# Regrouping the blocks of a feed-forward layer that is woven into a gather loop

## The chip, the cores and the metric

The kernel runs on one core of one Trainium2 chip. The metric is device time in microseconds (us) of one execution, compared as the median of several runs; less is better. TensorE (PE in the profile) multiplies matrices, with its weight loads shown apart (PEld); VectorE is DVE, ScalarE is ACT, GpSimd is POOL, and SyncE is SP. Each engine works through its own queue in order, and semaphores tie the queues together.

## The reference, cut to what matters

Two layers, each a graph convolution and a mixture of experts with residuals, run over 6,250 nodes of 256 features and 100,000 edges. Only the second layer ("layer 1") is touched:

```python
x = x + _L1_gnn_ref(edge_index, _layernorm(x), edge_type_8, L1_gnn_weight, ...)   # sum over the edges
# of a node: hx[edge_type, src], plus a loop term
x = x + _L1_ffn_ref(_layernorm(x)[None], ...)
# _L1_ffn_ref, per node: rh = relu(f @ router_w1 + b); p = softmax(rh @ router_w2 + b)
#   top 2 of 6 experts, their p put through a second softmax
#   expert e: relu(relu(f @ w1[e] + b1) @ w2[e] + b2) @ w3[e] + b3, all matrices 256 x 256
#   output: the two chosen experts, weighted
```

The kernel computes all six experts for every node, and weights those not chosen with zero.

## The kernel before, in words

The 6,250 nodes lie in 49 blocks of 128. X (the features) and acc (the sums of the graph convolution) stay in the on-chip memory for all 49 blocks. The stages follow one another: the edges are sorted into tiles, layer 0's convolution and experts run, the table hx of layer 1 (each node times eight relation matrices, as three bf16 parts) is written to HBM, and then layer 1's last stage runs, which is the one that the change touches.

**The gather loop.** `aggregate` (L801) takes T = 830 turns. In each, POOL issues one indirect DMA (L815) that fetches 128 rows of hx into one of ten buffers g; PE multiplies them, in three matmuls (L823), with a 0/1 matrix m that DVE builds once for eight turns (L807); DVE adds the product to the block of acc (L827). Edges are ordered by their target, so blocks become complete one after another: by the bound that the program uses, block b is complete at turn 17 x (b+1) + 8 (TURNS = 17, SLACK = 8).

**The feed-forward, woven in.** `aggregate` is a generator that yields once per turn, and `layer1` (L1395) uses each yield to put other work in the queues. The 49 blocks are split into groups by SIZES (L48); before the change these are a group of 2, eleven groups of 4, a group of 2 and a group of 1. A group passes through two generators:

- `prepare` (L1306), about one step per yield: residual and statistics of a block (L1313, L1317, one block per step), the inverse root (L385 to L392), normalising and transposing (L1329, L416, L418), the router's first product pq (L1339, with ACT's relu into q, L1341), the router's second product pl (L1346), softmax, the choice of two and the second softmax, a chain of some 25 small DVE rows with two exponentials on ACT (L1351, L865 to L897) that ends in the weights C, the transposes pc of C (L1360) with ACT's copy cT (L1362), and one product pcb per block that adds the weighted last bias (L1367, L1368). For four blocks this is 24 steps, for two 19, for one 15 or so.
- `experts1` (L1373): for each of six experts, two hidden products of two halves (L428, tiles ph_e1 and ph_e2, each half a piece, followed by ACT's relu, L435), and then `mix` (L904, L905), a product py for each block with the weighted add to X, two blocks to a piece. So an expert has 4 pieces plus one per two blocks: 36 pieces in a group of four, 30 in a group of two and also in a group of one.

A group's preparation may begin when its last block is complete and fewer than two groups wait in `queue`. Pieces of the experts are dealt out by a running account: each turn adds left / (T - turn + 40) to `due`, capped at 1.5, and a piece is issued for each whole unit; `left` begins as the pieces of all groups but the last two. When `queue` is empty no piece can be issued. After turn 830 what is left is issued at full rate, one step and one piece at a time.

**Order.** Every engine's queue is fixed when the program is built. A transpose, pq, pl or pc stands in PE's one queue among the gather's matmuls and the pieces, and if its input is late, everything behind it waits.

The same loop is built twice: the branch with names ending in b is for inputs with uneven blocks, the branch with names ending in a is the one that this input takes (all tiles of the trace end in a).

Of the kernel before, what the change touches and what calls it, by code (L numbers as in the profile page):

```python
# [44 lines left out]
TABLE_GROUPS = [(0, 1)] + [(g, 4) for g in range(1, NT, 4)]  # L45

LIVE = 3
SIZES = [2] + [4] * 11 + [2, 1]  # L48
FFN_GROUPS = [(sum(SIZES[:i]), n) for i, n in enumerate(SIZES)]


@with_exitstack
def gnn_ffn_kernel(ctx: ExitStack, tc: tile.TileContext, a, out):
# [747 lines left out]
    def aggregate(pool, acc, table, tag):  # L801

        for t0 in range(0, TL, 8):
            n = min(8, T - t0)
            blocks = blocks_of(blkd, t0, [ENG.DVE], NT)
            m = pool.tile([128, 8, 128], BF16, name=f"m1{tag}_{t0}", tag="m", bufs=2)
            nc.vector.tensor_tensor(  # L807
                m[:, :n],
                lanes_h[:, None, :].to_broadcast([128, n, 128]),
                dlocT[:, t0 : t0 + n, None].to_broadcast([128, n, 128]),  # L810
                OP.is_equal,
            )
            for j in range(n):
                g = pool.tile([128, 3 * D], BF16, name=f"g1{tag}_{t0 + j}", tag="g", bufs=10)
                nc.gpsimd.indirect_dma_start(  # L815
                    out=g,
                    out_offset=None,
                    in_=table,
                    in_offset=bass.IndirectOffsetOnAxis(ap=idxT[:, t0 + j : t0 + j + 1], axis=0),
                )  # L820
                ps = psum_mm(f"pa1{tag}_{t0 + j}")
                for k in range(3):
                    nc.tensor.matmul(  # L823
                        ps[:, :D], m[:, j, :], g[:, k * D : (k + 1) * D], start=(k == 0), stop=(k == 2)
                    )
                here = acc[:, bass.ds(blocks[j] * D, D)]
                nc.vector.tensor_add(here, here, ps[:, :D])  # L827
                yield t0 + j + 1
# [544 lines left out]
    def experts1(g, n, va, tag, xT, C):  # L1373

        tiles = range(g, g + n)
        m = n * 128
        for e in range(6):
            h1 = va.tile([128, 2, 512], F32, name=f"v1{tag}_{g}_{e}", tag="actT", bufs=1)
            h2 = va.tile([128, 2, 512], F32, name=f"v2{tag}_{g}_{e}", tag="hid", bufs=1)
            b1 = [col("L1_ffn_expert_b1", 2 * e + f) for f in range(2)]  # L1380
            b2 = [col("L1_ffn_expert_b2", 2 * e + f) for f in range(2)]
            yield from dense_steps(f"e1{tag}_{g}_{e}", vw1[:, e], xT, m, AF.Relu, b1, h1)
            yield from dense_steps(f"e2{tag}_{g}_{e}", vw2[:, e], h1, m, AF.Relu, b2, h2)
            for i, t in enumerate(tiles):
                mix(f"1{tag}", t, i, e, C, h2, i * 128, vw3[:, e])
                if e == 5:
                    r = last if t == NT - 1 else 128
                    nc.sync.dma_start(out[t * 128 : t * 128 + r, :], X[:r, t, :])
                if i % 2 or i == n - 1:
                    yield  # L1390

    def pieces(n):
        return 6 * (4 + (n + 1) // 2)

    def layer1(tag, early):  # L1395


        with tc.tile_pool(name=f"gather{tag}", bufs=1) as gp, tc.tile_pool(name=f"act{tag}", bufs=1) as va:
            waiting = list(FFN_GROUPS)
            prep, queue = None, []  # L1400
            left = sum(pieces(n) for _, n in waiting[:-2])

            def prepare_some():

                nonlocal prep
                if prep is None:
                    return False
                g, n, steps = prep
                try:
                    next(steps)  # L1410
                except StopIteration as end:
                    queue.append(experts1(g, n, va, tag, *end.value))
                    prep = None
                return True

            def experts_some():
                while queue:
                    if next(queue[0], queue) is not queue:
                        return True
                    queue.pop(0)  # L1420
                return False

            due = 0.0
            for turn in aggregate(gp, acc, hx, tag):
                if not early:
                    continue
                if prep is None and waiting and len(queue) < LIVE - 1 and TURNS * sum(waiting[0]) + SLACK <= turn:
                    g, n = waiting.pop(0)
                    prep = (g, n, prepare(g, n, va, tag))
                prepare_some()  # L1430
                due = min(due + left / (T - turn + 40), 1.5)
                while due >= 1 and experts_some():
                    due, left = due - 1, left - 1
            while prep or waiting or queue:
                if prep is None and waiting and len(queue) < LIVE:
                    g, n = waiting.pop(0)
                    prep = (g, n, prepare(g, n, va, tag))
                prepare_some()
                experts_some()

    nlate_v = nc.values_load(nlate[0:1, 0:1], min_val=0, max_val=NT, skip_runtime_bounds_check_because="it is a count")
    with tc.If(nlate_v > 0) as late_cmp:
        layer1("b", False)
    with late_cmp.Else():
        layer1("a", True)
# [56 lines left out]
```

## Time and profile before

| what | value |
|---|---|
| median of 3 runs | 4212.74 us (4209.37 to 4214.22) |
| the profiled execution, its own time | 4220.04 us |
| its span, first to last instruction | 4218.3 us |
| busy, PE / PEld / DVE / ACT / POOL | 3288.1 / 2125.4 / 2072.4 / 1168.6 / 2307.8 us |
| mean granted TensorE clock | 0.883 |
| first and last gather of layer 1 issued (L815) | 2955.8 and 4095.2 us |
| last add of the gather loop (L827) begins | 4110.1 us |
| last product of the experts (L904) begins | 4212.3 us |
| PE busy, DMA share, stretch 3300 to 3400 us | 99.76 of 100 us, 0.55 |

Busy times are of one profiled execution, which was 7.3 us above the median. A row of a list of instructions gives its start and its duration; xN means N records merged in the row. A float32 product leaves two records, so a 128x512 half of a hidden layer (two products) is x4. In brackets stand the idle time of the engine before the row and what ended it.

### The profile page before, as it was taken

The numbers are of one execution on the slowest core, as the hardware profiler recorded it, in microseconds if no ns is written. First come the engines' busy times: TensorE is split into PE (matmuls) and PEld (weight loads), VectorE is DVE, ScalarE is ACT, GpSimd is POOL, SyncE is SP. The second block draws the span as 40 slices with busy tenths as digits, with TensorE's granted clock in tenths as the row PEclk, the third lists the DMA queues.
The fourth block names the chain that finished last, engine by engine and source line by source line (L and its number), as shares of the span: only waits on it lengthen the run. The fifth ranks groups of instructions, "written<-read, shape, count | busy, mean of one in ns | idle before, by whom it ended". The sixth has DMA issues, their size and how long they took to land.

```text
span 4218.3 us, 49934 instructions
## 1 busy us (share of the span) xinstructions
PE 3288.1 (78%) x13207; PEld 2125.4 (50%) x13207; DVE 2072.4 (49%) x5527; ACT 1168.6 (28%) x2569; POOL 2307.8 (55%) x2488
## 2 busy tenths in 40 slices
PE   2886555565555559999749977999679999999999
PEld 1565444444444335554537743444256666666656
DVE  5676200000000058888563357665456666666652
ACT  3312433333333300000434433665012222222213
POOL 1000777777777755555470048333767777777750
PEclk9998877767777779999769988999589999999999
DMA  4413433333333356666333335444655555555540
GB/s 169 155 43 110 153 124 121 123 123 120 121 122 122 108 190 230 225 227 209 106 115 107 109 105 201 194 194 205 190 142 151 152 151 153 150 155 150 146 117 9
DMA packets 235392, 611.60 MB, mean 145 GB/s; under 512 B 44269, under 2 KB 128482, under 8 KB 215139
## 3 DMA queue, kind: packets, MB, share of 16 engines
q0 software_dynamic: 102928, 294.81, 22.5%
q1 hardware_dynamic: 105200, 234.80, 16.6%
q10 hardware_dynamic: 26976, 78.69, 5.4%
q8 instruction: 115, 1.88, 0.2%
q14 instruction: 173, 1.42, 0.1%
HBM read 371.46 MB, written 243.18 MB: 146 GB/s over the span
## 4 chain that ended last, share of the span: by engine, by line
PE 42%; DVE 10%; POOL 4%; issue 3%; DMA 3%; ACT 2%; DVEq 1%; SPq 0%; POOLq 0%; ACTq 0%
PE ph_e1a L428 6%; PE py1a L904 6%; PE pa1a L823 5%; PE pa L797 5%; PE ph_e2a L428 5%; PE phx L1265 4%; DVE acc L799 3%; PE pf L1184 2%; PE pf L1200 2%; POOL m L795 2%; DVE rest L1275 1%; PE pg L989 1%; DVE acc L827 1%; PE pt_fh L416 1%; DVE hx L1259 1%
## 5 line engine op out<-in xcount | busy, mean ns | idle before, releaser
L764 POOL DMA_INDIRECT msgs<-msg,at x830 | 833.1, 1004 | 599.2 <-ACT msg L761 388.6
L815 POOL DMA_INDIRECT g1a<-hx,idxT x830 | 826.6, 996 | 321.1 <-PE pa1a L823 148.0
L758 PE MATMUL px<-acc,sT 128*128 x1660 | 601.4, 541 | 481.7 <-ACT msg L761 447.6
L758 PEld LDWEIGHTS px<-acc,sT 128*128 128x128 f32 x1660 | 459.3, 284 | 623.1 <-ACT msg L761 487.6
L761 ACT ACTIVATE msg<-px,ewT 128x256 f32<-128x256 f32 x830 | 356.7, 474 | 697.1 <-DMA msgs<-msg,at 568.6
L827 DVE TENSOR_TENSOR acc<-acc,pa1a 128x256 f32 x830 | 346.6, 418 | 341.7 <-PE pa1a L823 311.1
L797 PE MATMUL pa<-g,m 128*128 128x256 f32 x1660 | 448.2, 419 | 84.5 <-DVE m L787 44.7
L823 PE MATMUL pa1a<-g1a,m1a 128*128 128x256 bf16 x2490 | 376.4, 283 | 51.9 <-DMA g1a<-hx,idxT 37.2
L1265 PE MATMUL phx<-wr,xT 128*128 128x512 f32 x784 | 371.7, 618 | 29.2 <-DVE rest L1275 22.8
L797 PEld LDWEIGHTS pa<-g,m 128*128 128x128 f32 x1660 | 249.5, 189 | 283.5 <-issue 114.8
L795 POOL TENSOR_SCALAR m<-lanes,key 128x128 f32<-128x128 f32 x414 | 263.2, 651 | 229.0 <-PE pa L797 206.4
L799 DVE TENSOR_TENSOR acc<-acc,pa 128x256 f32 x830 | 348.2, 419 | 73.6 <-PE pa L797 6.0
L823 PEld LDWEIGHTS <-m1a 128*128 128x128 bf16 x2490 | 243.2, 100 | 277.3 <-issue 191.7
L755 DVE COPY msg<-srcT 128x32 f32<-128x32 f32 x104 | 18.8, 182 | 700.2 <-DMA msgs<-msg,at 700.0
L904 PE MATMUL py1a<-w_L_ffn_expert_w,v2a 128*128 128x256 f32 x1176 | 286.6, 384 | 6.0 <-DVE acc L827 3.0
L428 PE MATMUL ph_e1a<-xT3a,w_L_ffn_expert_w 128*128 128x512 f32 (+2 forms) x672 | 288.0, 555 | 0.0
L428 PE MATMUL ph_e2a<-v1a,w_L_ffn_expert_w 128*128 128x512 f32 (+2 forms) x672 | 280.1, 542 | 2.1 <-DVE acc L827 1.3
L1225 POOL DMA_INDIRECT y<-ys,ats x98 | 98.0, 1000 | 298.3 <-DMA ys<-fy 272.5
L435 ACT ACTIVATE v1a<-ph_e1a,cols 128x512 f32<-128x512 f32 (+2 forms) x168 | 106.5, 634 | 538.7 <-PE ph_e1a L428 538.6
L1265 PEld LDWEIGHTS phx<-wr,xT 128*128 128x128 f32 x784 | 149.1, 198 | 189.6 <-issue 163.4
L904 PEld LDWEIGHTS py1a<-w_L_ffn_expert_w,v2a 128*128 128x128 f32 x1176 | 208.8, 190 | 44.2 <-ACT v2a L435 10.1
L753 DVE TENSOR_SCALAR sT<-rows,part 128x1024 f32<-128x1024 bf16 x104 | 83.8, 808 | 236.0 <-PE px L758 233.5
(610 smaller groups left out, 4285.6 us busy)
## 6 DMA issues: line engine op xcount, KB each, us to landing
hx<-hx SPq DMA_DIRECT2D x49, 1536.0 KB, 5.0
g<-msgs SPq DMA_DIRECT2D x52, 1040.0 KB
g<-msgs ACTq DMA_DIRECT2D x52, 1040.0 KB, 4.9
rows<-lane_rows SPq DMA_DIRECT2D x104, 256.0 KB, 3.6
fx<-xs SPq DMA_DIRECT2D x105, 128.0 KB, 2.0
ys<-fy ACTq DMA_DIRECT2D x105, 128.0 KB
msgs<-msg,at POOLq DMA_INDIRECT x830
g1a<-hx,idxT POOLq DMA_INDIRECT x830
```

The lines of the kernel that those rows point to most:

```text
L428: nc.tensor.matmul(ps[:, :ncols], w[:, k, f * 128 : (f + 1) * 128], xT[:, k, :ncols], start=(k == 0), stop=(k == 1),)
L758: nc.tensor.matmul(ps[:, :D], sT[:, j, :], acc[:, bass.ds(blocks[j] * D, D)], start=True, stop=True)
L761: nc.scalar.activation(msg[:, j, :D], ps[:, :D], AF.Copy, scale=ewT[:, t0 + j : t0 + j + 1])
L764: ins = nc.gpsimd.indirect_dma_start(out=msgs, out_offset=bass.IndirectOffsetOnAxis(ap=at[:, t0 + j : t0 + j + 1], axis=0), in_=msg[:, j, ...
L795: nc.gpsimd.tensor_scalar(m[:, j], lanes, key[:, j : j + 1], None, op0=OP.is_equal)
L797: nc.tensor.matmul(ps[:, :D], m[:, j, :], g[:, j, :D], start=True, stop=True)
L799: nc.vector.tensor_add(here, here, ps[:, :D])
L815: nc.gpsimd.indirect_dma_start(out=g, out_offset=None, in_=table, in_offset=bass.IndirectOffsetOnAxis(ap=idxT[:, t0 + j : t0 + j + 1], axi ...
L823: nc.tensor.matmul(ps[:, :D], m[:, j, :], g[:, k * D : (k + 1) * D], start=(k == 0), stop=(k == 2))
L827: nc.vector.tensor_add(here, here, ps[:, :D])
L904: nc.tensor.matmul(ps[:, :D], hT[:, k, j : j + 128], w[:, k, :], start=(k == 0), stop=(k == 1))
L1265: nc.tensor.matmul(ps, xT[:, k, :], wr[:, k, r : r + 2, :].rearrange("p r o -> p (r o)"), start=(k == 0), stop=(k == 1),)
```

## The change

The groups become 1, 2, 2, 3, then nine of 4, then 2, 2 and 1: sixteen groups where there were fourteen. And in a turn in which a step of a preparation was taken while `queue` holds no group, a second step is taken.

```diff
-SIZES = [2] + [4] * 11 + [2, 1]
+SIZES = [1, 2, 2, 3] + [4] * 9 + [2, 2, 1]
...
                 if prep is None and waiting and len(queue) < LIVE - 1 and TURNS * sum(waiting[0]) + SLACK <= turn:
                     g, n = waiting.pop(0)
                     prep = (g, n, prepare(g, n, va, tag))
-                prepare_some()
+
+                if prepare_some() and not queue:
+                    prepare_some()
                 due = min(due + left / (T - turn + 40), 1.5)
                 while due >= 1 and experts_some():
                     due, left = due - 1, left - 1
```

`left` begins at 480 where it was 426, since small groups have more pieces for the same blocks.

## Prediction

> **What bounds the kernel now.** I read the page's slices first, for where PE is full:
>
> ```profile
> PE   2886555565555559999749977999679999999999
> ...
> POOL 1000777777777755555470048333767777777750
> ...
> PEclk9998877767777779999769988999589999999999
> ```
>
> Each digit is a tenth of a 105 us slice. The last 12 slices are layer 1's gather loop. In its first two slices PE is at 6 and 7 and the granted clock at 5 and 8; in the other ten both are at 9. POOL is at 6 or 7 and ends one slice before PE. So PE bounds the stage except at its head. The stretches (busy us of PE, PEld, DVE, ACT, POOL, then PE's clock, DMA share, GB/s) say by how much:
>
> ```profile
> core 0: us, PE busy (x) PEld busy (x) DVE busy (x) ACT busy (x) POOL busy (x), PEclk, DMA share, GB/s
> ...
> 2950.00:3000.00 50.00, 24.70 (x93) 9.44 (x93) 17.97 (x34) 0.00 (x0) 34.16 (x34) 0.50 0.78 248
> 3000.00:3050.00 50.00, 31.77 (x126) 16.37 (x127) 25.68 (x84) 4.15 (x9) 36.65 (x39) 0.59 0.56 154
> ...
> 3200.00:3300.00 100.00, 99.53 (x472) 62.99 (x471) 63.41 (x169) 20.83 (x34) 73.49 (x74) 1.00 0.54 151
> ...
> 4050.00:4100.00 50.00, 44.87 (x193) 26.86 (x192) 26.43 (x90) 9.05 (x17) 25.48 (x26) 0.90 0.41 118
> ...
> 4150.00:4219.00 69.00, 60.15 (x292) 46.91 (x290) 13.14 (x41) 21.71 (x53) 0.00 (x0) 0.98 0.04 14
> ```
>
> From 2955.8 us (first gather) to about 3150, PE is half idle and much of it at half clock; from 3200 on it is full; near 4075 it loses 5 us, and 9 in the last 69. What sets the pace at the head is POOL:
>
> ```profile
> 3019.78 0.95 POOL L815 DMA_INDIRECT g1a<-hx,idxT  x1 [0.30 <-issue]
> 3021.03 0.94 POOL L815 DMA_INDIRECT g1a<-hx,idxT  x1 [0.30 <-issue]
> ```
>
> The start-to-start of the gathers is 1.25 us (0.95 busy, 0.30 issue), whatever PE does. At turn 251 the 250 turns before have taken 350 us: gather 251 is issued at 3296.4, its add begins at 3306.2.
>
> **A price list for PE.** At full clock, from rows of full stretches: the three gather matmuls 0.35 us per turn; a float32 record of 128x512 0.4325, of 128x256 0.216 (128x384 by proportion, 0.324). Per block and expert that is 2.59 us, and 15.6 for six; preparation adds 1.6 per block. Laying out PE's queue by turns and pricing each row gives 817 us for turns 151 to 750 of before, which took 818.5. I count in this list and in time lost against it. Before: 1134.1 of work in the stage, and from 2955.8 to the last product's start near 4212.5 some 123 lost, nearly all of it (107) before turn 251.
>
> **Work added.** Two more groups. Their extra DVE rows (about 30 of 0.17 us each, 5 us per group), ACT relus and weight loads (0.19 us each) lie beside PE, which is the full one (DVE 63%, ACT 21%). Uncovered, DVE's would cost 10. On PE only the second group of one costs more per block:
>
> ```profile
> 4185.96 1.89 PE L428 MATMUL ph_e1a<-xT3a,w_L_ffn_expert_w 128*128 128x256 f32 x8
> 4187.68 1.92 PE L428 MATMUL ph_e2a<-v1a,w_L_ffn_expert_w 128*128 128x256 f32 x8
> 4189.74 1.99 PE L904 MATMUL py1a<-w_L_ffn_expert_w,v2a 128*128 128x256 f32 x8
> 4191.57 1.05 PE L428 MATMUL ph_e1a<-xT3a,w_L_ffn_expert_w 128*128 128x128 f32 x8
> 4192.69 1.16 PE L428 MATMUL ph_e2a<-v1a,w_L_ffn_expert_w 128*128 128x128 f32 x8
> ```
>
> In the first three rows a group of two takes 5.61 us per expert (three phases, 4185.96 to 4191.57), of which the list has 5.19; in the last two a group of one, with 128 columns, starts its next phase after 1.12 us for 8 records, 0.14 each and not 0.108. So a group of one costs 6 x (16 x 0.14 + 0.87) = 18.7 against 15.6: **+3.2**. The Trainium skill ("TensorE: Matmul & The Clock Gate", section "Wait — 56ns, not 53.3ns?") has warm matmuls start N / 2.4 GHz plus 2.5 ns apart, which would make the short records nearly proportional and this term about 0.3; the measured row decides. Gathers, SP's stores and POOL's queue keep their number and order.
>
> **The head, turns 1 to 250.** The experts now begin at turn 32 instead of 60, and the 17 turns without a piece (116 to 132), where before waited 29 us, go. But the account deals out pieces, not work. It gives 0.57 pieces per turn (480/838), and a piece is worth 18.7/30 = 0.62 us in a group of one, 1.04 in a group of two, 46.7/36 = 1.30 in the group of three, 1.73 in a group of four. So PE's load per turn is 0.35 + 0.57 x 0.62 = 0.70, then 0.94, then 1.09, each plus about 0.1 of preparation: under POOL's 1.25 until the group of three ends, at turn 250. PE cannot be filled there, POOL paces it. Gather 251 then comes at 2955.8 + 250 x 1.25 = 3268, plus delays of the gathers that no buffer explains (5.6 us in the first 125 turns of before, so 11) = 3279, and its add 10 later (3306.2 - 3296.4 in before) = 3289 to 3290. **-16.** Bounds: -23 if add follows gather by 4 us, as it does where PE waits for data, and 0 if short pieces hold PE back (a rival below). In these turns the list has 234.3 us of work after and 243.5 before, as a piece is smaller; so 9.2 is put off, and with the 3.2: **+12.4** behind turn 250.
>
> **The double step** acts only with the queue empty: in the first group (8 turns instead of 15, where POOL paces anyway) and in the gaps below. There the same DVE chain must finish with fewer gather turns standing between pl and pc; PE waits for the chain either way. I take 0, between -2 and +2 for each gap.
>
> **The gaps.** After turn 250 the account is faster than the blocks: a group of four is dealt out in 36/0.573 = 63 turns, but four blocks take 4 x 17 = 68 turns to become complete. The queue runs dry, with turns without a piece: 3 before turn 506, 4 before 572, 6 before 639, 6 before 705, 8 before 772. Before has 2 or 3 up to turn 609, then 4 (677), 4 (745), 6 (813). What such a gap costs is in the trace; the one of 6:
>
> ```profile
> 4053.58 1.88 PE L428 MATMUL ph_e1a<-xT3a,w_L_ffn_expert_w 128*128 128x512 f32 x4
> ...
> 4063.59 0.95 PE L1346 MATMUL pl3a<-qw,qa 128*128 128x6 f32 x8
> ...
> 4074.44 0.18 DVE L897 TENSOR_TENSOR C1a<-oh_1a,oh_1a 128x24 f32<-128x24 f32 x1
> 4074.68 0.60 PE L1360 MATMUL pc1a<-ident,C1a 128*6 128x128 f32 x4 [4.04 <-DVE C1a L897]
> ...
> 4075.94 1.35 PEld L1367 LDWEIGHTS pcb1a<-vb,cT1a 6*128 6x128 f32 x4 [0.96 <-ACT cT1a L1362]
> ...
> 4081.31 3.62 PE L428 MATMUL ph_e1a<-xT3a,w_L_ffn_expert_w 128*128 128x512 f32 x4
> ```
>
> pl ends at 4064.4, its chain on DVE gives C only 10 us later, and pc stands in PE's queue in front of the gathers and experts that wait: 4.04 us idle, 0.67 for cT (in its row), and then half clock: pcb 2.07 for 1.13, e1 3.62 for the 1.88 of the first row. Together with the second pcb and two gather turns at half clock: 9. The gap of 4 at 745:
>
> ```profile
> 3976.16 0.31 PEld L1360 LDWEIGHTS pc1a<-ident,C1a 128*6 128x6 f32 x4 [1.90 <-DVE C1a L897]
> ...
> 3980.49 3.40 PE L428 MATMUL ph_e1a<-xT3a,w_L_ffn_expert_w 128*128 128x512 f32 x4
> ```
>
> 1.62 and 0.66 idle, and e1 at 3.40: 4. The gap of 4 at 677 cost nothing, as two ph_e2 and two py pieces stood between pl and pc (9 us of cover).
>
> The cover decides, and PE's new order shows it. Before turn 506: two ph_e2 and four py halves between pl and pc, covered, 0. Before 572: the same queue as before 813, 8. Before 639: pl after the last py, only five gather turns between (1.75) against a chain of 6.3 (5.8 at 3873 with few adds between its rows, 10 above): 4.5 + 0.7 + 3.5 of clock = 9. Before 705: two turns, 5.6 + 0.7 + 3.5 = 9.5. Before 772: the transposes too are late, for the normalised blocks: about 2 more idle and pq at half clock, 13. Sum 39.5, against 13 before: **+26** (from +8, if half of each is hidden, to +40 if all chains take 10). In the row at 3980 the clock is halved after 2.3 us of idle. The skill (same page, "HAM oscillation — how this bites in real kernels") has it fall only for idle gaps over about 3.4 us; by the page the gap before 572 might keep its clock and the sum be 3 lower.
>
> **The tail.** The loop ends with 26 of 30 pieces of a group of two, and a two and a one, instead of 24 of 36 of a four, a two and a one. The work is in the list; the waits for ACT between phases, 0.42 per expert of a two, now come 11 times, not 6: **+2**.
>
> Sum: -16 + 12.4 + 26 + 2 = +24. The profiled execution's 4220.04 becomes 4244; it lay 7.3 above the median, so on the median of 4212.74 I forecast 4237.
>
> **Rivals.** *Faster:* the head keeps POOL's bare pace (-22) and the double step lets the chains end under the gather turns, so that the gaps cost 10 in all, 3 less than before: -22 + 12.4 - 3 + 2 = -11, 4202. It decides for faster once the gaps cost under 12 with the head at -22. For it: 116 to 132, the worst stall of before, is certainly removed. Against: 6 us of chain against 0.7 to 2 of cover.
>
> *No change:* gaps as at 745, 4 each, one covered: 16, so +3, and the head at -16: +1, 4214.
>
> *Slower still:* short pieces at half clock hold PE behind POOL. A piece of a group of one, four records at twice 0.14, is then 1.1 us; the 1.7 gather turns to a piece, at twice 0.35, are 1.2; and where before ran a group of two (3055 to 3110) PE waited some 0.56 for ACT after many a piece. That is 2.9 us against 2.1 of POOL, and over the group's 30 pieces 23 late, of which the ten buffers take up 7 (add 11 behind gather instead of 4). The head then gains nothing, 4253, or 6 if the clock rises half way, 4247.
>
> That the other branch runs is excluded by the names of the trace.
>
> **How the numbers follow.** Forecast 0.58 (its own range 4222 to 4247), slower still 0.12, no change 0.17, faster 0.13. 0.2% is 8.4 us, about what a measurement of this kernel can tell from no change. Faster by more than that: 0.13; within it: 0.17 and the low edge of the forecast, 0.19; slower: 0.68. The range that leaves out a tenth at each end goes from the faster rival, 4202, to 4257, where the head gains nothing and the gaps cost 4 more.
>
> **What would show it.** Right: add 251 near 3290; PE under 90% busy up to about turn 250; pc rows with 4 to 6 us idle before C, followed by e1 rows near 3.4, four of them between turns 565 and 775; the last gather later than 4095, near 4130, and a tail after it shorter by about 15. Wrong: PE full between turns 560 and 775, or no half-clock rows there; or a gather pace above 1.3 us before turn 250.

## The result, and the profile after

The changed kernel takes 4258.32 us (median of 5 runs, 4254.02 to 4259.44), the kernel before 4212.74 on the same chip: a ratio of 1.0105 (95% interval 1.0093 to 1.0117), 45.6 us slower. The forecast was 4237, slower, in a range from 4202 to 4257; the median lies 1.3 us above that range's upper end. The sign held, but the loss forecast, 24 us, was about half of the one that came. All experiments below ran on three other chips, where the kernel before takes 4528.58 us (e1 to e4), 4499.84 (e5 to e8) and 4532.24 (e9 to e12), so they are read as ratios to the kernel before on their own chip.

The page's slices of the changed kernel, each digit a tenth of a 106 us slice:

```profile
PE   2886655555555469997859968997689999999999
...
POOL 1000777777777755554650067334777766766650
...
PEclk9998777777776789999869989998799999999999
```

The last 12 slices are again layer 1's loop and tail. PE's first two are at 6 and 8, and the clock's at 7 and 9, where before had 6 and 7, 5 and 8: PE has more work in the head, at a higher clock. The other ten are at 9, as before, so the slices are too coarse to show what was lost. The stretches show it (busy us of PE, PEld, DVE, ACT, POOL; clock, DMA share, GB/s):

```profile
core 0: us, PE busy (x) PEld busy (x) DVE busy (x) ACT busy (x) POOL busy (x), PEclk, DMA share, GB/s
2950.00:3000.00 50.00, 24.81 (x104) 11.67 (x104) 23.19 (x59) 2.23 (x4) 38.48 (x37) 0.56 0.76 240
3000.00:3050.00 50.00, 32.76 (x189) 23.57 (x189) 27.38 (x85) 6.59 (x19) 37.50 (x37) 0.81 0.51 144
3200.00:3300.00 100.00, 91.82 (x477) 61.31 (x476) 62.33 (x167) 20.03 (x39) 77.17 (x76) 1.00 0.55 154
4050.00:4100.00 50.00, 42.56 (x179) 25.14 (x177) 25.08 (x75) 8.56 (x16) 24.30 (x27) 0.86 0.39 110
4150.00:4200.00 50.00, 48.79 (x238) 39.04 (x237) 25.52 (x115) 16.90 (x41) 0.00 (x0) 1.00 0.07 21
4200.00:4257.00 57.00, 48.13 (x248) 39.17 (x246) 8.64 (x19) 17.30 (x44) 0.00 (x0) 0.97 0.02 7
```

From 3000 PE now has 189 matmuls in 50 us where it had 126, at a clock of 0.81 where it was 0.59: experts start early, as the change says. But 3200 to 3300, full before (99.53), is at 91.82, and 4050 to 4100 loses 7.4 us with the clock at 0.86. The stretches behind 4150 are the tail.

Cut at the adds of turns 251 and 826, the two profiled executions differ so (us; "work" and "lost" by the prediction's price list):

| stretch | before | after | difference |
|---|---|---|---|
| start to first gather | 2955.8 | 2950.5 | -5.3 |
| first gather to add of turn 251 | 350.4 | 347.1 | -3.3 |
| add 251 to add 826 | 797.2 | 859.9 | +62.7 |
| of it work | 785.8 | 815.6 | +29.8 |
| of it lost | 11.4 | 44.4 | +33.0 |
| add 826 to the end of the span | 114.9 | 99.0 | -15.9 |
| span | 4218.3 | 4256.5 | +38.2 |

The "work" is an estimate by that list. The last 7.3 us of the 45.6 are no part of this: the profiled execution of before lay 7.3 above its median, that of after on it.

**The gaps.** Who held PE up between the two adds, from the waits of PE (total us, times, longest), first of before, then of after:

```profile
PE pc1a L1360 <- DVE C1a L897: 5.7, 2, 4.0
PE pcb1a L1367 <- ACT cT1a L1362: 1.3, 2, 0.7
```

```profile
PE pc1a L1360 <- DVE C1a L897: 19.6, 5, 5.7
...
PE pcb1a L1367 <- ACT cT1a L1362: 2.7, 4, 0.7
```

Four of the five waits behind pc are the gaps of the prediction, before turns 572, 639, 705 and 772: 3.16, 4.67, 5.72 and 5.22 us. The list of PE's instructions at the third of them:

```profile
3950.27 1.06 PE L1346 MATMUL pl3a<-qw,qa 128*128 128x6 f32 x8
3951.19 1.03 PE L823 MATMUL pa1a<-g1a,m1a 128*128 128x256 bf16 x8
3957.94 1.01 PE L1360 MATMUL pc1a<-ident,C1a 128*6 128x128 f32 x4 [5.72 <-DVE C1a L897]
3959.62 2.07 PE L1367 MATMUL pcb1a<-vb,cT1a 6*128 6x256 f32 x4 [0.67 <-ACT cT1a L1362]
...
3964.37 3.78 PE L428 MATMUL ph_e1a<-xT3a,w_L_ffn_expert_w 128*128 128x512 f32 x4
...
3968.59 2.53 PE L428 MATMUL ph_e1a<-xT3a,w_L_ffn_expert_w 128*128 128x512 f32 x4
```

The gather matmuls behind pl end at 3952.2, then PE stands 5.72 us in front of pc, until DVE has C. Then come 0.67 for cT, and rows at half clock: pc 1.01 for 0.60, pcb 2.07 for 1.13, the first e1 3.78 for 1.88, and even the second is at 2.53. By the list the 25 turns around each gap lost 8.9, 8.4, 12.6 and 13.9 us: 43.8 of the 44.4 lost between the two adds.

**The head.** The waits in PE's list in the first 250 turns, of before (groups of 2 and 4):

```profile
3026.61 1.11 PE L416 MATMUL pt_x3a<-ident,xn3a 128*128 128x128 f32 x4 [4.13 <-DVE xn3a L1329]
...
3040.36 0.59 PE L1360 MATMUL pc1a<-ident,C1a 128*6 128x128 f32 x2 [3.93 <-DVE C1a L897]
...
3123.72 2.30 PE L416 MATMUL pt_x3a<-ident,xn3a 128*128 128x128 f32 x8 [3.83 <-DVE xn3a L1329]
...
3140.51 1.02 PE L1360 MATMUL pc1a<-ident,C1a 128*6 128x128 f32 x4 [4.53 <-DVE C1a L897]
```

and of after (groups of 1, 2 and 2; the 3 follows):

```profile
2992.55 0.69 PE L416 MATMUL pt_x3a<-ident,xn3a 128*128 128x128 f32 x2 [2.96 <-DVE xn3a L1329]
...
3003.54 0.38 PE L1360 MATMUL pc1a<-ident,C1a 128*6 128x128 f32 x1 [5.66 <-DVE C1a L897]
...
3048.96 1.11 PE L416 MATMUL pt_x3a<-ident,xn3a 128*128 128x128 f32 x4 [3.31 <-DVE xn3a L1329]
...
3066.09 0.59 PE L1360 MATMUL pc1a<-ident,C1a 128*6 128x128 f32 x2 [2.74 <-DVE C1a L897]
...
3097.98 0.73 PE L416 MATMUL pt_x3a<-ident,xn3a 128*128 128x128 f32 x4 [2.87 <-DVE xn3a L1329]
```

A preparation holds PE up for the normalised block (pt) and again for C (pc), 2.7 to 5.7 us each in these rows, and that of one block (2.96 and 5.66) as long as that of four (3.83 and 4.53). After has four such preparations in the head, where before had two that held PE up. In all, PE waits 26.1 us in preparation rows in 16 places, and 18.7 in 9 before.

### The profile page after: what moved, and what is told of

It reads as the page before. It is cut to its first block, busy times and chain, and to the rows that moved or that the text cites. A ratio compares the mean times of both kernels' runs of the same rounds, so it can differ in the third digit from the quotient of the medians.

```text
span 4256.5 us, 50483 instructions
## 1 busy us (share of the span) xinstructions
PE 3300.8 (78%) x13407; PEld 2162.9 (51%) x13407; DVE 2080.8 (49%) x5601; ACT 1183.8 (28%) x2625; POOL 2302.1 (54%) x2488
## 3 DMA queue, kind: packets, MB, share of 16 engines
q0 software_dynamic: 102928, 294.81, 22.2%
## 4 chain that ended last, share of the span: by engine, by line
PE 40%; DVE 11%; DMA 4%; issue 4%; POOL 3%; ACT 2%; DVEq 1%; SPq 0%; ACTq 0%; POOLq 0%
PE ph_e1a L428 6%; PE pa1a L823 5%; PE pa L797 5%; PE ph_e2a L428 5%; PE py1a L904 5%; PE phx L1265 3%; DVE acc L799 3%; PE pf L1184 2%; PE pf L1200 2%; POOL m L795 2%; DMA g1a<-hx,idxT 2%; DVE rest L1275 1%; DVE acc L827 1%; PE pt_fh L416 1%; DVE hx L1259 1%
## 5 line engine op out<-in xcount | busy, mean ns | idle before, releaser
L758 PE MATMUL px<-acc,sT 128*128 x1660 | 605.8, 544 | 477.7 <-ACT msg L761 444.0
L428 PE MATMUL ph_e1a<-xT3a,w_L_ffn_expert_w 128*128 128x512 f32 (+3 forms) x768 | 294.8, 511 | 1.6 <-DVE X L905 0.5
L428 PE MATMUL ph_e2a<-v1a,w_L_ffn_expert_w 128*128 128x512 f32 (+3 forms) x768 | 285.0, 497 | 0.9 <-ACT v1a L435 0.4
L435 ACT ACTIVATE v1a<-ph_e1a,cols 128x512 f32<-128x512 f32 (+3 forms) x192 | 112.6, 587 | 580.9 <-PE ph_e1a L428 567.2
L905 DVE SCALAR_TENSOR_TENSOR X<-py1a,C1a,X 128x256 f32<-128x256 f32 x294 | 139.6, 481 | 128.4 <-PE py1a L904 127.6
```

What stands on the lines that cost most here:

```text
L428: nc.tensor.matmul(ps[:, :ncols], w[:, k, f * 128 : (f + 1) * 128], xT[:, k, :ncols], start=(k == 0), stop=(k == 1),)
L758: nc.tensor.matmul(ps[:, :D], sT[:, j, :], acc[:, bass.ds(blocks[j] * D, D)], start=True, stop=True)
```

## The experiments

A summary first. "Dry" are the spells of 3 turns or more without a piece behind turn 251, from PE's order. The two waits are those of PE in front of pc for DVE between the adds of turns 251 and 826, and in front of any preparation row (pt, pq, pl, pc, pcb) for DVE or ACT before the add of turn 251; each is the sum from the waits of PE in that stretch, with the number of places. Waits for which the profile shows no releaser are left out; the largest is one of 7.3 us in front of pc in e4.

| kernel | ratio to before (95%) | dry, turns | behind pc, 251 to 826 | preparations, head |
|---|---|---|---|---|
| before | 1 | 3, 3, 4, 4, 6 | 5.7 (2) | 18.7 (9) |
| changed | 1.0105 (1.0093 to 1.0117) | 3, 4, 6, 6, 8 | 19.6 (5) | 26.1 (16) |
| e1 | 1.0034 (1.0021 to 1.0047) | 4, 7, 9, 12 | 17.6 (3) | 29.2 (17) |
| e2 | 1.0093 (1.0076 to 1.0111) | none | 0.5 (1) | 33.4 (16) |
| e3 | 1.0033 (1.0021 to 1.0044) | 3 | 1.7 (1) | 32.5 (17) |
| e4 | 1.0057 (1.0041 to 1.0074) | 6, 6, 7, 8, 9, 9, 12, 15 | 36.5 (8) | 23.8 (7) |
| e5, changed again | 1.0062 (1.0045 to 1.0078) | 3, 4, 6, 6, 8 | 20.1 (5) | 36.4 (18) |
| e6 | 0.9989 (0.9977 to 1.0002) | none | 0.2 (1) | 27.4 (8) |
| e7, as e2 | 1.0095 (1.0075 to 1.0115) | none | 0.5 (1) | 34.0 (18) |
| e8 | 1.0068 (1.0050 to 1.0085) | none | 1.8 (2) | 29.2 (12) |
| e9 | 1.0035 (1.0022 to 1.0049) | none | 1.1 (2) | 43.8 (18) |
| e10 | 0.9983 (0.9975 to 0.9992) | none | 0.8 (2) | 20.2 (8) |
| e11 | 1.0031 (1.0019 to 1.0043) | none | 1.1 (2) | 36.5 (16) |
| e12 | 1.0090 (1.0075 to 1.0105) | 5, seven of 3 or 4 | 19.6 (5) | 32.3 (11) |

Two things can be read down the columns. A queue that runs dry for 7 turns or more, or that runs dry several times with the second step in force, costs 17.6 to 36.5 us behind pc; that of the kernel before, with 6 at most and one step, 5.7; one that does not run dry, or for 3 turns once, 0.2 to 1.8. And fronts of 1, 2, 2, 3 wait in 16 to 18 places in the head, fronts of 2 and 4 in 7 to 9 (11 with the second step, 12 with a second group of two).

### The parts of the change: e1, e12 and e5

e1 has the sizes without the second step:

```diff
-SIZES = [2] + [4] * 11 + [2, 1]
+SIZES = [1, 2, 2, 3] + [4] * 9 + [2, 2, 1]
```

Expected (e1 to e4 give us on the median of 4212.74):

> The new sizes without the second step per turn. Gap theory (the loss is PE waiting behind pc for a late router chain whenever the experts' queue has run dry): the gaps without a piece become 4, 7, 9 and 12 turns (before turns 575, 643, 711, 779) instead of 3, 4, 6, 6 and 8, but a gap costs its chain and its half clock, not its turns, so about 8 + 10 + 11 + 13 = 42 us against the 44 measured with the second step; the first group begins at turn 40 and not 32. Total 4250 to 4266. Rival A (the second step is what costs): 4225 to 4240, at most half the loss left. Rival B (the second step earns much): above 4270.

Measured 4547.78, a ratio of 1.0034. As ratios the expectations are 1.0088 to 1.0127 for the theory of the gaps and 1.0029 to 1.0065 for Rival A, so the result is Rival A's: the second step costs. But the changed kernel, too, loses less away from the first chip (e5), so that the theory of the gaps is not refuted by the size alone; its waits behind pc are there, 17.6 us in three places.

e12 has the second step with the sizes of before:

```diff
-                prepare_some()
+                if prepare_some() and not queue:
+                    prepare_some()
```

> The kernel before with the second step of a preparation while no experts are due, and nothing else. Its queue then runs dry ten times: 14 turns before turn 121, 7 before 195, 5 before 266, seven times 3 or 4 later. Theory (the second step is worth nothing by itself, a chain must finish either way): the 6 and 4 turns at the end shrink to 4 and 3 (up to -8), the gaps at 195 and 266 cost 4 to 8 each: -4 to +10, ratio 0.999 to 1.0025. Rival (the step is what costs the changed kernel, as it takes the cover from between pl and pc): +12 to +25, ratio 1.003 to 1.006.

Measured 4572.96, 1.009, some 41 us more than before: far above both. The list of PE's instructions at the gap before turn 335, of 3 turns:

```profile
3652.46 0.95 PE L1346 MATMUL pl3a<-qw,qa 128*128 128x6 f32 x8
...
3658.37 1.99 PE L904 MATMUL py1a<-w_L_ffn_expert_w,v2a 128*128 128x256 f32 x8
3660.20 1.15 PE L823 MATMUL pa1a<-g1a,m1a 128*128 128x256 bf16 x9
3665.37 0.93 PE L1360 MATMUL pc1a<-ident,C1a 128*6 128x128 f32 x4 [4.02 <-DVE C1a L897]
3666.97 2.07 PE L1367 MATMUL pcb1a<-vb,cT1a 6*128 6x256 f32 x4 [0.67 <-ACT cT1a L1362]
...
3671.72 3.78 PE L428 MATMUL ph_e1a<-xT3a,w_L_ffn_expert_w 128*128 128x512 f32 x4
```

Here the last py pieces of the group are out before pc, and the second step has brought pc to the third turn without a piece: behind the last piece stand only three gather turns, 1.15 us, and pc waits 4.02, with e1 at half clock behind it. In the kernel before, at its gap of 3 turns before 609, pc stands among the last py products and waits for nothing. So the step acts exactly where no piece is left to cover the chain, and it makes the dry spells more: eight behind turn 251 for five. The 19.6 us behind pc are under half of the 41; the kernel before was not profiled on this chip, so the rest is not traced.

e5 is the changed kernel again, unchanged:

> The changed kernel itself again, beside the kernel before, so that it and the three others have runs of the same chip. Expected: 1.0105 of the kernel before, as measured; in the trace from turn 251 to 825 about 44 us lost against the price list, and about 347 us from the first gather to the add of turn 251. If the ratio is nearer to 1 here, the change's cost depends on the pace that the gathers have on the chip.

Measured 4529.39, 1.0062. Its pc waits are those of the first profile:

```profile
PE pc1a L1360 <- DVE C1a L897: 16.1, 3, 5.7
```

(4.0 more have other DVE rows of the same chain as their releaser, so 20.1 in all.) The ratio is smaller than 1.0105, so what the change costs depends on the chip. Against e6 on the same chip, the kernel before with a filled queue, its span is 35.5 longer: start -1.8, head +29.4, turns 251 to 826 +26.7, tail -18.8. There the head costs what it did not on the first chip, and the middle costs less, since the kernel with a filled queue also loses there (105.9 us by the list, where before on the first chip lost 11.4). By the list some 26 of the 26.7 are work put off and added, so between the two adds e5 with its gaps lost as much as e6 without any: on this chip the gaps are there and cost nothing that can be told. e5 less e1 (0.0028, with half-widths of 0.0013 and 0.0017, on two chips) points to some 13 us for the second step inside the change; that is no clean comparison.

### Filling the queue: e3, e6, e4 and e9

e3 is the changed kernel with a slower account, e6 the kernel before with one:

```diff
-                due = min(due + left / (T - turn + 40), 1.5)
+                due = min(due + 0.92 * left / (T - turn + 40), 1.5)     # e3; 0.93 in e6
```

> The changed kernel with the account slowed to 0.92 of its pace; sizes and second step as changed. The gaps before 506, 572, 639 and 705 go, one of 3 turns stays before 777. Gap theory: -38 for the gaps, up to +8 for work put off in the head where PE had room: 4220 to 4230. Rival (the experts are simply late in the head, and a slower pace puts off more): 4265 or more.

> The kernel before, with the account of pieces multiplied by 0.93, so that the queue does not run dry before turns 745 and 813. Theory of the gaps (a dry queue makes PE wait behind pc for the chain on DVE, and half clock follows): the 13 us lost there go, a few pieces are left for the tail, so 8 to 14 us less than before, ratio 0.997 to 0.998. Rival (a pace that is lower leaves the work for the tail, where it costs as much): ratio 1.000 to 1.003. In the trace the first theory wants the half-clock e1 rows after pc gone.

Both took the waits behind pc away (1.7 and 0.2 us). e3 measured 1.0033, what the theory of the gaps said as a ratio; but e1, on the same chip, has 17.6 us of these waits and the same time (4547.78 and 4547.95). By the list e3 has 5.1 us more work between the adds, and lost 61 between turns 251 and 550, where e1 lost 38: without gaps it loses elsewhere on this chip. e6 measured 0.9989 (0.9977 to 1.0002), less gain than the 0.997 to 0.998 expected, and not told from none.

One thing limits all tests of the gaps on these chips. From the add of turn 251 to that of turn 550 e1, e2, e5, e7 and e9 take 463.2 to 464.0 us, although by the list PE has some 20 us less work there in e2 and e7, which deal fewer pieces per turn, than in e1 and e5. So PE's work does not set the pace of these turns there, and a piece that is put off saves nothing in them. On the first chip, where PE had next to no idle time, the changed kernel took 425.4 us for them and the kernel before 407.5. What sets the pace on the others is not shown.

e4 does the reverse and makes the spells longer: the sizes of before with groups of two at the end, one more than the change has.

```diff
-SIZES = [2] + [4] * 11 + [2, 1]
+SIZES = [2] + [4] * 10 + [2, 2, 2, 1]
```

> The sizes of before with the last group of 4 split into 2 and 2, no second step, nothing changed at the head. The account now leaves out 2 + 1 blocks of a list that has 30 more pieces and so deals 0.56 per turn: gaps of 6, 6, 6, 7, 8, 9, 9, 12 and 15 turns from turn 201 on, behind the one of 20 at turn 133. Gap theory: each of the nine costs 8 to 14 us, together about 95 against the 15 that the gaps of before cost, so 4280 to 4310, although less than 0.1% of PE's work is new. Rival (what costs is the small groups at the head): within 10 us of before.

Measured 1.0057: slower, with eight waits behind pc and 36.5 us in them, the most of all. The direction is that of the theory, not the rival's (within 10 us); the size is under half of what the theory gave.

e9 fills the changed kernel's queue without a constant: a turn gets at most the pieces in hand divided by the turns until the next group can follow (the lines that count pieces and steps, h[1] and prep[3], are left out).

```diff
...
-                due = min(due + left / (T - turn + 40), 1.5)
+                rate = left / (T - turn + 40)
+                hand = sum(h[1] for h in queue)
+                if prep is not None:
+                    rate = min(rate, hand / max(prep[3], 1))        # prep[3]: steps still to come
+                elif waiting:
+                    ahead = max(0, TURNS * sum(waiting[0]) + SLACK - turn) + steps_of(waiting[0][1])
+                    rate = min(rate, hand / ahead)
+                due = min(due + rate, 1.5)
```

> The changed kernel with its pieces spread: the account gives per turn at most the pieces in hand divided by the turns until the next group can follow, so that the queue never runs dry after its first piece. Same sizes, same second step. Theory of the gaps: the 33 us that the changed kernel lost behind pc between turns 251 and 825, over what the kernel before lost there, go; 5 us of work move to the tail: about 28 us less than the changed kernel, ratio to the kernel before 1.002 to 1.004 where the changed kernel has 1.0105, and 0.997 to 1.003 where it has 1.006. Rival (the gaps only show where PE waits, POOL's pace would have cost the same): the ratio of the changed kernel, 1.006 or more. Theory of the head: what is left over the next kernel comes in the first 250 turns.

Measured 1.0035; the waits behind pc are 1.1. With e3 that is twice the same answer: where the changed kernel has 1.0062, it has about 1.0034 with a filled queue, some 13 us less. That points to a gain and does not show it: the three ratios are of three chips, each against its own runs of before, and the intervals of e5 and e9 touch. What remains with a filled queue is not gaps.

### The head: e2, e7, e8, e10 and e11

e2 and e7 are one kernel: the changed front and the second step, no groups of two at the end.

```diff
-SIZES = [1, 2, 2, 3] + [4] * 9 + [2, 2, 1]
+SIZES = [1, 2, 2, 3] + [4] * 10 + [1]
```

> The same head (1, 2, 2, 3) and the second step, but then ten groups of 4 and a 1. The account leaves out the last two groups, here 4 + 1 blocks instead of 2 + 1, so it deals 0.537 pieces per turn and not 0.573: a group of four takes 67 turns, its blocks 68, and there is no turn without a piece between groups. Gap theory: the 44 us of the gaps go and the head stays as it is: 4212.7 + 3 (second group of one) + 6 (head, in which the changed kernel lost 113 us against 107) - 15 (the gaps of before) - 2 (no group of two in the tail) = 4205, range 4195 to 4220. Rival (small groups at the head are what costs, by stalls that go on): 4235 or more.

> Groups of 1, 2, 2 and 3 at the front, then ten of four and one of one, with the second step: the changed front and the double step without the groups of two at the end. Theory of the head (four small preparations at the head each hold PE up by their DVE chains, so the head gains 3 us and not 16) with the theory of the gaps (their phase comes from the groups at the front, and this order of sizes has three short ones of 3 turns at most): work put off +9, head -3, gaps 0 in place of 13, second group of one away: -7 to +5, ratio 0.998 to 1.001. Rival (the front itself carries the loss by what it puts off, gaps or not): ratio 1.006 to 1.009.

Measured 1.0093 and 1.0095, on two chips: the largest loss of the experiments, without a single gap, and a plain miss of both expectations' first theory. The numbers are the rivals' (1.0053 or more; 1.006 to 1.009). On one chip e7's span is 41.8 longer than e6's: head +17.6, turns 251 to 826 0.0, tail +24.1. The expectation forgot the tail: with an end of 4 and 1 the list has 132.1 us of work behind turn 825, with the ends of the others 87 to 107. e8 shows the same with a front of 2 and 2:

```diff
-SIZES = [2] + [4] * 11 + [2, 1]
+SIZES = [2, 2] + [4] * 11 + [1]
```

> The kernel before with groups 2, 2, eleven of four and 1: the same number of groups, the group of two moved from the end to the front; no second step. Its queue never runs dry after turn 250. Theory of the gaps: 13 us lost go, the start stays as before (one group of two, then another in place of a group of four: the 17 turns without a piece shrink), the tail changes by a few us: 15 to 25 us less than before, ratio 0.994 to 0.9965. Rival (short groups at the head cost what they save): 0.998 to 1.002.

Measured 1.0068, above both theories; its span against e6: start +5.2, head +7.6, middle -11.6, tail +22.2. A front with one group under four more costs 7.6 in the head, one with three more, and the second step in the first of them (e7), 17.6.

e10 is the nearest pair to e9, on the same chip: the front of before, the end of the change with one more group of two, the spread account, one step per turn. (In e9 the second step is taken only in the first group, turns 25 to 32, as the queue is not empty later.)

```diff
-SIZES = [2] + [4] * 11 + [2, 1]
+SIZES = [2] + [4] * 10 + [2, 2, 2, 1]
...
                 prepare_some()
+                rate = ...                                          # as in e9
```

> The front of the kernel before (2, then groups of four), the end of the changed one (2, 2, 2, 1), one step per turn, pieces spread as in the run before. Theory of the gaps: the 13 us of the kernel before behind pc go, the 17 turns without a piece before turn 133 are filled (up to 10), the tail has 12 us less work and the loop 12 more: 15 to 25 us less than before, ratio 0.994 to 0.997. Theory of the head: it is 10 to 30 us shorter than the spread changed kernel on the same chip, nearly all before turn 251. Rivals: the front costs nothing and both are within 5 us; or the end split costs what it saves, ratio 0.999 to 1.003.

Measured 4523.57, 0.9983 (0.9975 to 0.9992). It is the one kernel that beats both, by 8.7 us on the medians, less than the 15 to 25 expected. Against e9 it is 23.9 shorter on the medians, and 19.7 by the spans, of which the head has 23.7 (428.5 against 404.8, with 8.4 us less work by the list in the slower one), the start 2.4, the middle -7.5 and the tail 1.1. Three of PE's waits in the head, of e9:

```profile
PE pt_x3a L416 <- DVE xn3a L1329: 24.5, 6, 12.5
...
PE pa1a L823 <- ACT v2a L435: 15.7, 13, 3.1
PE pc1a L1360 <- DVE C1a L897: 15.4, 4, 5.7
```

and of e10 (which has another 3.2 behind pc, with C1a as the releaser):

```profile
PE pt_x3a L416 <- DVE xn3a L1329: 11.6, 3, 8.4
PE pa1a L823 <- ACT v2a L435: 8.5, 8, 3.4
...
PE pc1a L1360 <- DVE km1a0b L840: 3.9, 1, 3.9
```

All of PE's waits for DVE and ACT in preparation rows, and elsewhere for ACT's relus, come to 68.7 us in e9 and 34.0 in e10. This difference of 34.7 is about as large as the 32 us by which the two heads differ when the work is taken off. It is no full account: PE's whole idle time in the two heads, 428.6 - 300.0 and 404.8 - 295.0 us, differs by 18.8 only, since e10 waits longer for the adds (24.4 us against 8.0), and the rest are rows that ran longer in e9. POOL shows where the waits go: before gather 251 it is idle 163.6 us in e9 and 140.7 in e10, and most of this difference are buffers that PE's gather matmuls held (91.2 and 73.5 us). So small preparations at the head cost in two ways: their own chains, and, as far as these sums go, more phases that wait for ACT.

e11 asks whether the half clock is behind it: e9 with three idle matmuls ahead of each of the first 100 turns' own, overwritten by them.

```diff
+                for k in range(3 if t0 + j < 100 else 0):
+                    nc.tensor.matmul(ps[:, :D], m[:, j, :], m[:, 0:2, :], start=True, stop=True)
                 for k in range(3):
                     nc.tensor.matmul(
```

> The spread changed kernel with three more matmuls ahead of each of the first 100 turns' gather matmuls, from the matrix m alone and overwritten by the real ones: 35 us of work for PE where it waits for gathers. Theory (half clock makes the short pieces of the head slow): the granted clock of the first 130 us rises towards 1, the time from the first gather to the add of turn 251 falls by 8 to 20 us, ratio 0.002 to 0.005 lower than without. Rival (the preparations' chains on DVE, the waits for ACT and PE's own order hold the head): no shorter, up to 15 us longer.

Stretches 3180 to 3280 of e9, and then of e11 (the clock is the third figure from the end):

```profile
3180.00:3230.00 50.00, 31.37 (x170) 22.78 (x170) 20.96 (x60) 6.47 (x18) 30.54 (x30) 0.76 0.41 116
3230.00:3280.00 50.00, 32.34 (x154) 22.82 (x153) 25.07 (x82) 6.09 (x15) 29.87 (x30) 0.76 0.42 119
```

```profile
3180.00:3230.00 50.00, 35.75 (x243) 28.11 (x242) 20.55 (x57) 5.99 (x16) 28.53 (x28) 0.90 0.38 108
3230.00:3280.00 50.00, 39.02 (x270) 30.79 (x267) 26.61 (x86) 7.21 (x19) 31.91 (x32) 0.97 0.45 129
```

The clock rose from 0.76 and 0.76 to 0.90 and 0.97, with 35 us of added work that found room; the way from the first gather to the add of turn 251 went from 428.5 to 431.4 us, and the ratio from 1.0035 to 1.0031, within the intervals. The half clock in the head costs no more than this work did, which is not shown to be free: the rival with the chains stands, and the price of the half clock alone stays open.

## Why the prediction was right and wrong

**The sum.** Forecast +24 on the spans, measured +38.2. Term by term: the work put off and added +12.4, measured 29.8 - 17.3 = +12.5 (the list has 104.8 us of work behind turn 825 before, 87.5 after); the tail's waits +2, measured +1.4 (-15.9 + 17.3); the gaps +26, measured +33.0; the head -16, measured -3.3; and -5.3 before the first gather, which no term had and which no run explains. The 7.3 us between profile and median was taken for something that both executions would have, and belonged to one. Up to the first gather the two programs are the same, so the 5.3 may be part of the 7.3; that is not shown. Head +12.7, gaps +7.0, execution +7.3, start -5.3 and tail -0.6 make the 21 us by which 4237 was short.

**The step that failed is the head**, "PE cannot be filled there, POOL paces it". It took 1.25 us per gather and 11 us of delays. The gathers of the changed kernel are 1.36 apart up to turn 251 (3290.9 - 2950.5 over 250), which the prediction itself listed as a sign against it, and so were those of before (3296.4 - 2955.8): the delays are 28 us in both, not 11. POOL's busy time from the first gather to gather 251 says what they are, before and then after (window, its length, POOL's busy us and gathers, clock, DMA share, GB/s):

```profile
2955.80:3296.30 340.50, 249.35 (x250) 0.84 0.56 161
```

```profile
2950.50:3290.90 340.40, 255.32 (x250) 0.88 0.56 161
```

At 0.946 us, the median, 250 gathers take 236.5; in the changed kernel 18.8 us more lie in gathers that ran long (up to 2.01), in the kernel before 12.9. The other 9 and 15 are idle time above 0.30 per gather, nearly all for buffers that PE held:

```profile
3070.22 0.94 POOL L815 DMA_INDIRECT g1a<-hx,idxT  x1 [3.85 <-PE pa1a L823]
...
3104.34 0.94 POOL L815 DMA_INDIRECT g1a<-hx,idxT  x1 [2.87 <-PE pa1a L823]
```

These two, the longest, follow PE's waits at 3066 (pc) and 3098 (pt) shown above. So the 17 turns without a piece went, but PE still held POOL up behind its preparations. The text counted PE's work in the preparations (0.1 us per turn), and not their chains, though two of these stood in the trace of before at 3026 and 3040. It also took the gathers' own long rows for 11 us; why there are more of them after the change no run shows. The 3.3 us that the head gained are those by which the add follows gather 251 sooner (6.6 for 9.9). The prediction's rival *Slower still* had the outcome for the head (nothing gained) by another mechanism, the half clock, which e11 speaks against on its chip. On the first chip PE's idle time in the head grew by 12.6 us (347.1 - 271.1 against 350.4 - 287.0), of which 7.4 stand in preparation rows and 5.9 in front of gather matmuls whose data was late (43.1 for 37.2).

**The gaps** were where they were said to be, four between turns 565 and 775 and none at 506, with the idle time as forecast: 5.72 and 0.67 before 705 for 5.6 and 0.7. The term that was too small is the clock behind them: at 705 the rows run long up to the second e1 (2.53), which adds up to about 5.5 us and not 3.5. So 12.6 there against 9.5, and 13.9 against 13 at 772; 639 with 8.4 against 9 and 572 with 8.9 against 8 were met. The upper end of the range stood for a head that gains nothing and gaps that cost 4 more, which is nearly what came. In the prediction's two fences on gaps the rows of pcb at 4075.94 and of pc at 3976.16 are those of the weight loads; the 0.67 and 1.62 of its text are the waits of the matmuls that belong to them.

**The clock.** At the gap before 572 the list of PE's instructions shows

```profile
3756.10 0.60 PE L1360 MATMUL pc1a<-ident,C1a 128*6 128x128 f32 x4 [3.16 <-DVE C1a L897]
3757.36 1.23 PE L1367 MATMUL pcb1a<-vb,cT1a 6*128 6x256 f32 x4 [0.66 <-ACT cT1a L1362]
...
3761.27 3.78 PE L428 MATMUL ph_e1a<-xT3a,w_L_ffn_expert_w 128*128 128x512 f32 x4
```

3.16 us of idle, 0.66 more, and e1 at 3.78 for 1.88. The Trainium skill ("TensorE: Matmul & The Clock Gate", "HAM oscillation — how this bites in real kernels") keeps the clock up to idle gaps of about 3.4 us. Here it was halved behind shorter gaps, as at 3980 of before (1.62 and 0.66 us idle), so the measured rows decide, and the gap cost 8.9 where 8 were forecast.

**The double step**, taken as 0, is wrong as a step: alone it costs about 41 us (e12, on another chip). The reason given, that PE waits for the chain either way, holds only where nothing covers the chain in any case. At a gap of 3 turns there was cover, and the step took it away.

**The tail** was 15.9 us shorter for 15 forecast, and the last gather came later, at 4149.0 for 4130, as the loop took up what the head and the gaps did not give.

**What stays open.** Why the other chips need 7% more for both kernels, and with that how much of the first chip's 45.6 us a filled queue would have given back there. That the gaps cost 33 us more there rests on the rows of one profile of each kernel; no experiment ran on that chip, and on the others a filled queue gave back 13 us at most. A version with the sizes of the change but neither gaps nor second step was not run.

## What to carry to other kernels

A small piece of work that sits in an in-order queue ahead of the main work costs by its latency and not by its size: splitting a group to start earlier multiplies the stalls, one chain per group, so count the groups and not only the blocks. When a planner deals out filler work, let its pace be bounded by what is in hand until more can come: a queue that runs dry exposes the next chain, and the halved clock behind it can cost as much again, as on the first chip, where PE was full; where something else sets the pace, filling the queue gains little. And speeding up a preparation when nothing covers it only brings its consumer forward into the wait.

## What the hardware showed that was not expected

On the chip of e5 PE stands longer in front of instructions for which the profile shows no releaser. PE's group with the longest waits (layer 0), of the same changed kernel on the first chip and then in e5 (busy us, mean ns, idle before, its main releaser):

```profile
L758 PE MATMUL px<-acc,sT 128*128 x1660 | 605.8, 544 | 477.7 <-ACT msg L761 444.0
```

```profile
L758 PE MATMUL px<-acc,sT 128*128 x1660 | 702.8, 561 | 506.3 <-issue 341.5
```

One matmul takes much the same, 544 and 561 ns; in front of them "issue" has 341.5 us in e5, where on the first chip ACT's result had 444.0. In the gather loop of e5 turns without any gap lost 4 to 10 us per 50 by the list, and on the first chip under 3 from turn 251 on.

A clock raised by 35 us of matmuls that nobody needs (0.76 to 0.97 in one stretch) did not make the head shorter: 428.5 and 431.4 us.

The gathers' own instructions on POOL, 0.946 us at the median, ran up to 2.01 us, and in the first 250 turns such rows cost 12.9 us in the kernel before and 18.8 in the changed one.
